# A macaron block on one core: the FFN weight prepared on VectorE alone, and the first five tiles' FFNs and values closer together

## The chip, the cores and the metric

The kernel runs on one core of one Trainium2 chip. The core has TensorE (PE, matrix products), VectorE (DVE), ScalarE (ACT) and GpSimd (POOL), and SyncE (SP), whose queue issues most transfers here. Each engine takes its instructions in the order in which they stand in its own queue and waits where an operand isn't ready. The metric is device time in microseconds of one launch; the smaller the better.

## The reference, cut to what matters

The input x has 4 batches of 4096 rows of 512 values, 16384 rows in all. Three residual steps follow one another:

```python
x = x + 0.5 * ffn(layernorm(x))
x = x + attention(layernorm(x))          # 16 heads of 32, each query sees 13 neighbouring keys
x = x + 0.5 * ffn(layernorm(x))
```

`ffn(x, w, b)` quantises both x and w before the product. Blocks of 32 neighbouring values get one scale, the largest absolute value over 7.5; each value over its scale goes to the nearest point of a six-bit floating grid (a tie to the lower one); the product is taken of grid point times scale. The FFN weight is 512 x 512, and both FFNs use the same one. Attention has a 1536 x 512 weight for query, key and value, a bias table of 25 offsets per head, and a 512 x 512 output weight.

## The kernel before

**Tiles and stages.** The 16384 rows are cut into 128 tiles of 128 rows. One tile goes through: the norm and quantisation for the first FFN (`quantised_norms`, kind "n1"), the first FFN and the attention norm (`first_half`), the values product (`values`), and later the output projection (`project_out`), the second quantised norm ("n3") and the second FFN (`second_half`). Four tiles make a group; per group and 128 columns there is an item m (128 of them): `project_qk`, `softmax`, `attend`. All products with a weight go through `product` (L146): 12 matmuls of 128 x 128 by 512, because both sides are held as a high and a low half in f16. The product names in the profile are pmf (FFN), pmv (values), pmqk (query and key), pmo (output), pmb (a bias through the output weight); ps and pv are the two attention products.

**What sets the order.** Stages are generators that are entered with `begin(slot, stage, rank)` in a list of numbered slots (L162); `run_slot` runs all that stand in one slot by rank, and each `yield n, rank` puts the rest of the stage n slots later. A tile has STEP = 7 slots. Tile t loads x at slot 7t-18, its first norm stands at 7t-10, its first half at 7t+5, its values at 7t+20; item m has its query and key products at 7m+38 and its softmax at 7m+42. From L779 on (`manual_schedule`) the order on each engine is the order in which the program is written. What stands ahead of that line, the setup up to the last FFN weight chunk and the first norms of tiles 0 to 2 (EARLY = 3), is put in order by a scheduler with a modelled timeline.

**The setup** (L629 to L872). SP loads the FFN weight `fw` in four chunks of 128 rows, the first x tiles, and 16 chunks `rows` of the other weights (order 8-11 value, 12-15 output, then query and key chunks in turns). ScalarE takes the sum of squares of every chunk. `powers(lo, hi)` makes from them, per weight, a power of two: a maximum on VectorE, a tiny transpose on TensorE (ptn), a maximum and a diagonal on VectorE, a tiny product on TensorE (pb), and some ten small integer operations on VectorE that end in `up` and `down`. For the FFN weight, `powers(4, 5)`; for the others, `powers(0, 4)` in slot 0.

The loop L745 prepares the FFN weight, chunk by chunk: VectorE makes wqh = fw / scale in f16; GpSimd makes wu = wqh times the high, then the low part of the scale, and VectorE takes each off fw; VectorE makes wq from the rest, adds wqh, breaks ties (`tie_to_lower`, L142 and L144); ScalarE rounds to fp8 (w8); GpSimd multiplies the scale back in (L766); ScalarE casts the high half, VectorE makes the low half (whlf, L769), and SP transposes it into `wt` (`put_weights`, L704). The 16 other chunks go through `put_scaled` (whl: ScalarE L784, VectorE L786, SP transpose) in the slots of L866. The FFN's products need all four FFN chunks, a values product the chunks 8-11, pmb (`attention_bias`, L813) the chunks 12-15.

**Buffers that matter here.** The high and low halves hlq (quantised norm) and hln (attention norm) have one buffer each (`hlp`, L100); whl and whlf share four; `ps_m`, the products' PSUM, has three. The bias table is built from `rd`, `shifted` and `mask`/`masks`, transfers on SP (L828 to L857).

Of the kernel before, what the change touches and what calls it, by code (L numbers as in the profile page):

```python
# [37 lines left out]
P = 128  # L38
# [12 lines left out]
QB = 32  # L51
# [13 lines left out]
def macaron_kernel(  # L65
# [66 lines left out]

    def blocks(t):
        return t.rearrange("p (n q) -> p n q", q=QB)

    def tie_to_lower(t):

        nc.vector.scalar_tensor_tensor(t, t, BELOW_ONE, t, ALU.mult, ALU.min)  # L142
        ti = t.bitcast(I32)
        nc.vector.tensor_scalar(ti, ti, 1, None, ALU.bitwise_or)  # L144

    def product(pm, lhs, rhs):  # L146

# [14 lines left out]
    def begin(slot, stage, rank=5):  # L162
        slots.setdefault(slot, []).append((rank, stage))
# [400 lines left out]

    F1, V, QK, SC, PV, OUT, F2 = 5, 2 * STEP + 6, 5 * STEP + 3, 6 * STEP, 8 * STEP + 3, 13 * STEP + 2, 12

    def add_bias(t, b):
        nc.gpsimd.tensor_tensor(xs[t], xs[t], b, ALU.add)  # L568

    def one(f, *args):  # L570
        f(*args)
        return
        yield
# [24 lines left out]

    for t in range(NT):
        k = t * STEP  # L600
        begin(k - 18, one(load, t), 0)
        enlist(k - 10, t, "n1")
        if not 0 < t < EARLY:
            begin(k - 11, one(moments, k - 10, t, "n1"), 1)
        begin(k + F1, first_half(t))
        begin(k + V, values(t))
        begin(k + F1, one(add_bias, t, half_ffn_b), 8)
        at = out_slot(t)
        begin(at - 5, one(add_bias, t, after_b), 8)
        enlist(at + 2, t, "n3")  # L610
        begin(at, project_out(t, at + 2))
        begin(at + 6 if t < LAST else second_slot(t) - 2, one(add_bias, t, half_ffn_b), 8)
        begin(second_slot(t), second_half(t))
    for slot in together:
        if slot >= EARLY * STEP - 10:
            begin(slot, quantised_norms(slot), 1)
    for m in range(n_items):
        k = m * STEP
# [10 lines left out]
    with tc.tile_pool(name="setup", bufs=1) as sp, tc.tile_pool(name="scratch", bufs=2) as scr:  # L629
# [8 lines left out]
        nc.gpsimd.memset(rp, 0.0)  # L638
        nc.scalar.dma_start(out=rp[:, QR - 1 : QR - 1 + NREL], in_=rpb)


        rows = {}

        sq = sp.tile([P, 5 * KC], F32, name="sq")
        first = min(slots)
        for slot in range(first, first + EARLY * STEP, STEP):
            run_slot(slot)
        for _ in quantised_norms(-10):
            pass
        chunks = (8, 9, 10, 11, 12, 13, 14, 15, 0, 4, 1, 5, 2, 6, 3, 7)  # L650
        for o in chunks:
            w, i = (qkv_w, o) if o < 3 * KC else (proj_w, o - 3 * KC)
            rows[o] = xp.tile([P, dim], F32, tag="x", name=f"rows{o}")
            nc.sync.dma_start(out=rows[o], in_=w[i * P : (i + 1) * P, :])
        for o in (*range(4 * KC, 5 * KC), *chunks):
            src = fw[:, o - 4 * KC, :] if o >= 4 * KC else rows[o]
            junk = scr.tile([P, dim], BF16, tag="junk", name=f"junk{o}")
            nc.scalar.activation(junk, src, AF.Square, accum_out=sq[:, o : o + 1])
        ptb = ps_m.tile([P, 512], F32, tag="mm", name="ptb")
        nc.tensor.transpose(ptb[:, : 3 * KC], b12, ident[: 3 * KC, : 3 * KC])  # L660
        bT = sp.tile([P, 3 * KC], F32, name="bT")
        nc.vector.tensor_copy(bT, ptb[:, : 3 * KC])
        b2 = sp.tile([P, 3 * KC], F32, name="b2")
        nc.vector.scalar_tensor_tensor(b2, bT, 2.0 ** -8, bT, ALU.mult, ALU.mult)
        nc.vector.tensor_tensor(sq[:, : 3 * KC], sq[:, : 3 * KC], b2, ALU.add)
        top5 = sp.tile([P, 5], F32, name="top5")
        up = sp.tile([P, 5], F32, name="up")
        down = sp.tile([P, 5], F32, name="down")
# [1 line left out]
        def powers(lo, hi):  # L670

            w = hi - lo
            nc.vector.tensor_reduce(
                top5[:, lo:hi], sq[:, lo * KC : hi * KC].rearrange("p (m c) -> p m c", c=KC),
                AX.X, ALU.max,
            )
            ptn = ps_m.tile([P, 512], F32, tag="mm", name=f"ptn{lo}")
            nc.tensor.transpose(ptn[:w, :P], top5[:, lo:hi], ident)
            most = sp.tile([w, 1], F32, name=f"most{lo}")
            nc.vector.tensor_reduce(most, ptn[:w, :P], AX.X, ALU.max)  # L680
            diag = sp.tile([w, w], F32, name=f"diag{lo}")
            nc.vector.tensor_scalar(diag, ident[:w, :w], most, 2.0, ALU.mult, ALU.mult)
            ones_w = sp.tile([w, P], F32, name=f"ones{lo}")
            nc.gpsimd.memset(ones_w, 1.0)
            pb = ps_m.tile([P, 512], F32, tag="mm", name=f"pb{lo}")
            nc.tensor.matmul(pb[:, :w], ones_w, diag, start=True, stop=True)
            e = sp.tile([P, w], I32, name=f"e{lo}")
            nc.vector.tensor_copy(e.bitcast(F32), pb[:, :w])
            nc.vector.tensor_scalar(e, e, 23, None, ALU.logical_shift_right)
            nc.vector.tensor_scalar(e, e, 131, None, ALU.add)  # L690
            nc.vector.tensor_scalar(e, e, 1, None, ALU.logical_shift_right)
            nc.vector.tensor_scalar(e, e, 97, None, ALU.max)
            u, d = up[:, lo:hi].bitcast(I32), down[:, lo:hi].bitcast(I32)
            nc.vector.tensor_scalar(u, e, -1, 264, ALU.mult, ALU.add)
            nc.vector.tensor_scalar(u, u, 23, None, ALU.logical_shift_left)
            nc.vector.tensor_scalar(d, e, -10, None, ALU.add)
            nc.vector.tensor_scalar(d, d, 23, None, ALU.logical_shift_left)

        powers(4, 5)
        nc.vector.tensor_scalar(cf, down[:, 4:5], 0.5 / XS, None, ALU.mult)  # L700
        nc.gpsimd.tensor_scalar(half_ffn_b, half_ffn_b, 0.5, None, ALU.mult)

        def put_weights(o, hl):
            return nc.sync.dma_start_transpose(  # L704
# [19 lines left out]
        for o in range(KC):  # L724
            nc.vector.tensor_reduce(
                w_abs[:, o * NB : (o + 1) * NB], blocks(fw[:, o, :]), AX.X, ALU.max,
                apply_absolute_value=True,
            )
        nc.vector.tensor_scalar(w_sc, w_abs, 1.0 / Q_MAX, None, ALU.mult)
        split_scale()  # L730
        nc.vector.scalar_tensor_tensor(w_abs, w_hi, -Q_MAX, w_abs, ALU.mult, ALU.add)
        nc.vector.scalar_tensor_tensor(w_abs, w_lo, -Q_MAX, w_abs, ALU.mult, ALU.add)
        nc.vector.scalar_tensor_tensor(w_sc, w_abs, 1.0 / Q_MAX, w_sc, ALU.mult, ALU.add)
        nc.vector.tensor_scalar(w_sc, w_sc, Q_EPS, None, ALU.max)
        nc.vector.reciprocal(w_r, w_sc)
        split_scale()
        w_back = small("w_back")
        nc.vector.tensor_scalar(w_back, w_sc, up[:, 4:5], F8_SCALE, ALU.mult, ALU.mult)

        def large(name, o, dt=F32):  # L740
            return scr.tile(
                [P, NB, QB], dt, tag=name, bufs=3 if name == "wu_" else KC, name=f"{name}{o}"
            )

        for o in range(KC):  # L745
            fwb = blocks(fw[:, o, :])

            def per(t):
                return bc(t[:, o * NB : (o + 1) * NB], QB)

            qh, q0 = large("wqh_", o, F16), large("wq0_", o)
            nc.vector.tensor_tensor(qh, fwb, per(w_r), ALU.mult)
            for i, b in enumerate((w_hi, w_lo)):
                u = large("wu_", f"{o}_{i}")
                nc.gpsimd.tensor_tensor(u, qh, per(b), ALU.mult)
                nc.vector.tensor_tensor(fwb, fwb, u, ALU.subtract)  # L756
            nc.vector.tensor_tensor(q0, fwb, per(w_r), ALU.mult)
            nc.vector.tensor_tensor(q0, q0, qh, ALU.add)
            q0f = q0.rearrange("p n q -> p (n q)")
            tie_to_lower(q0f)  # L760
            w8 = large("w8_", o, F8)
            nc.scalar.activation(
                w8.rearrange("p n q -> p (n q)"), q0f, AF.Copy, scale=1.0 / F8_SCALE,
                saturate=False,
            )
            nc.gpsimd.tensor_tensor(fwb, w8, per(w_back), ALU.mult)  # L766
            hl = scr.tile([P, 2, dim], F16, tag="whl", bufs=4, name=f"whlf{o}")
            nc.scalar.copy(hl[:, 0, :], fw[:, o, :])
            nc.vector.tensor_tensor(hl[:, 1, :], fw[:, o, :], hl[:, 0, :], ALU.subtract)  # L769
            put_weights(4 * KC + o, hl)  # L770

        for t in range(1, EARLY):
            moments(t * STEP - 10, t, "n1")
            for _ in quantised_norms(t * STEP - 10):
                pass

        ctx.enter_context(tc.manual_schedule())  # L779

        def put_scaled(o):
            s = up[:, o // KC : o // KC + 1]
# [10 lines left out]
        vb = sp.tile([P, KC], F32, name="vb")  # L793

        def scales():
            powers(0, 4)
            nc.vector.tensor_scalar(cp, sd[:, 2:3], sd[:, 3:4], 1.0 / XS, ALU.mult, ALU.mult)
            nc.vector.tensor_scalar(
                alpha, sd[:, 0:1], sd[:, 1:2], QSCALE * XS ** -2, ALU.mult, ALU.mult
# [62 lines left out]
                    masks[:, k : k + 1, :].to_broadcast([P, KC, KN]), ALU.mult, ALU.add,  # L862
                )

        begin(0, one(scales), 9)
        for slot, o in zip((2, 4, 5, 6, 10, 13, 16, 19, 21, 23, 25, 27, 29, 31, 33, 35), chunks):  # L866
            begin(slot, put_scaled(o), 9)
        begin(28, attention_bias(), 9)
        begin(26, one(put_table), 9)
        slot = first  # L870
        while slot < QK:
# [47 lines left out]
```

## Time and profile before

| | before |
|---|---|
| median of 3 runs | 2388.48 us (2378.66 to 2392.82) |
| the profiled execution, its own time | 2398.3 us |
| its span | 2396.5 us |
| TensorE busy | 2285.3 us, 95% |
| VectorE busy | 2020.8 us, 84% |
| GpSimd busy | 1990.2 us, 83% |
| ScalarE busy | 1329.8 us, 55% |
| first FFN product begins | 58.50 us |
| first query product begins | 107.18 us |

The page of a profile gives busy time by engine, the chain of work that ended last, and the costliest groups of instructions. A timeline lists one engine's instructions in order: start in us, duration in us, engine, line and operation, what is written and read, and in brackets how long the engine was idle before it and what ended that ("<-"). A transfer's row on SPq is its issue, not its landing; when it landed is read from who waited for it. Where two instructions follow one another without a gap, the rows overlap by some 0.08 us, so that the pace, start to start, is a little shorter than the duration.

### The profile page before, as it was taken

The numbers are of one execution on the slowest core, as the hardware profiler recorded it, in microseconds if no ns is written. First come the engines' busy times: TensorE is split into PE (matmuls) and PEld (weight loads), VectorE is DVE, ScalarE is ACT, GpSimd is POOL, SyncE is SP. The second block draws the span as 40 slices with busy tenths as digits, with TensorE's granted clock in tenths as the row PEclk, the third lists the DMA queues.
The fourth block names the chain that finished last, engine by engine and source line by source line (L and its number), as shares of the span: only waits on it lengthen the run. The fifth ranks groups of instructions, "written<-read, shape, count | busy, mean of one in ns | idle before, by whom it ended". The sixth has DMA issues, their size and how long they took to land.

```text
span 2396.5 us, 82360 instructions
## 1 busy us (share of the span) xinstructions
PE 2285.3 (95%) x35539; PEld 1118.5 (47%) x35539; DVE 2020.8 (84%) x3588; ACT 1329.8 (55%) x2080; POOL 1990.2 (83%) x2012
## 2 busy tenths in 40 slices
PE   0799999999999999999999999999999999999998
PEld 0344444444444444444444444444444444444443
DVE  8789888888888888888888888888888878888886
ACT  4466555555555555555555555555555555555542
POOL 5578888888888888888888888888888888888886
PEclk9899999999999999999999999999999999999999
DMA  5789788777777777777777778877777786777773
GB/s 153 143 151 155 159 164 159 159 148 151 150 155 158 158 142 150 148 155 156 164 147 149 148 159 161 156 159 146 150 151 158 158 158 131 149 150 152 137 116 108
DMA packets 925701, 360.59 MB, mean 150 GB/s; under 512 B 718876, under 2 KB 889752, under 8 KB 925336
## 3 DMA queue, kind: packets, MB, share of 16 engines
q1 hardware_dynamic: 924992, 354.79, 74.3%
q8 instruction: 278, 4.55, 0.8%
q10 hardware_dynamic: 344, 0.53, 0.1%
q14 instruction: 87, 0.71, 0.1%
HBM read 110.15 MB, written 67.29 MB: 74 GB/s over the span
## 4 chain that ended last, share of the span: by engine, by line
PE 92%; DVE 4%; issue 1%; DMA 1%; POOL 1%; ACT 1%; SPq 0%; DVEq 0%; POOLq 0%; ACTq 0%
PE pmqk L151 28%; PE pmf L151 26%; PE pmo L151 14%; PE pmv L151 14%; PE ps L437 7%; PE pv L507 3%; DVE fw L756 0%; DMA x<-hln 0%; DVE hlq L204 0%; DVE stn L180 0%; DVE whl L786 0%; DMA fw<-in_L_ffn_weight_dram 0%; DVE sc L239 0%; POOL yq L251 0%; DVE x L279 0%
## 5 line engine op out<-in xcount | busy, mean ns | idle before, releaser
L151 PE MATMUL pmf<-wt,xT 128*128 128x512 f16 x3048 | 703.2, 381 | 12.9 <-DMA xT<-hlq 10.3
L151 PE MATMUL pmqk<-x,wt 128*128 128x512 f16 x3072 | 709.3, 381 | 4.8 <-DMA x<-hln 4.6
L151 PEld LDWEIGHTS <-xT 128*128 128x128 f16 x3048 | 298.8, 98 | 377.1 <-DMA xT<-hlq 12.7
L151 PEld LDWEIGHTS <-wt 128*128 128x128 f16 x3072 | 290.6, 98 | 342.7 <-issue 10.4
L151 PE MATMUL pmo<-wt,ring 128*128 128x512 f16 x1536 | 360.5, 385 | 8.5 <-issue 8.5
L151 PE MATMUL pmv<-wt,x 128*128 128x512 f16 x1536 | 354.1, 380 | 4.9 <-DVE mvn L181 4.9
L246 POOL TENSOR_TENSOR yq<-yq,r 128x1024 f32<-128x1024 f32 (+1 forms) x141 | 246.7, 1750 | 131.1 <-DVE r L244 131.1
L568 POOL TENSOR_TENSOR x<-x,half_ffn_b 128x512 f32<-128x512 f32 x256 | 327.8, 1280 | 0.1
L279 DVE SCALAR_TENSOR_TENSOR x<-pmf,coef,x 128x512 f32<-128x512 f32 x256 | 179.7, 702 | 151.9 <-PE pmf L151 151.6
L534 ACT ACTIVATE ring<-pv 128x510 f16<-128x510 f32 (+8 forms) x224 | 82.6, 415 | 396.6 <-PE pv L507 396.6
L314 ACT CAST vt<-pmv 128x512 f16<-128x512 f32 x128 | 75.1, 587 | 389.2 <-PE pmv L151 389.2
L180 DVE BATCH_NORM_STATS2 stn<-x 128x6 f32<-128x512 f32 x384 | 265.4, 691 | 9.0 <-DMA x<-in_L_attn_x_dram 0.2
L251 POOL TENSOR_TENSOR yq<-q,sc 128x1024 f32<-128x1024 fp8e4 (+1 forms) x141 | 246.9, 1751 | 1.0 <-ACT q L249 1.0
L151 PEld LDWEIGHTS <-x 128*128 128x128 f16 x1536 | 150.7, 98 | 187.6 <-DMA x<-hln 5.4
L377 DVE SCALAR_TENSOR_TENSOR qk<-pmqk,qk_b,qk 128x512 f16<-128x512 f32 x256 | 190.7, 745 | 52.9 <-ACT qk L373 51.8
L151 PEld LDWEIGHTS <-ring 128*128 128x128 f16 x1536 | 141.6, 99 | 173.2 <-issue 19.9
L480 POOL TENSOR_TENSOR sf<-sf,total 128x714 f32<-128x714 f32 (+2 forms) x128 | 178.8, 1397 | 42.8 <-DVE total L478 22.9
L186 POOL TENSOR_SCALAR rsq<-mv 128x2 f32<-128x2 f32 (+1 forms) x141 | 130.0, 922 | 99.3 <-DVE mv L181 96.9
L249 ACT ACTIVATE q<-yq,nudge 128x1024 fp8e4<-128x1024 f32 (+1 forms) x141 | 150.3, 1066 | 112.0 <-POOL yq L246 103.8
L373 ACT ACTIVATE qk<-pmqk,qk_b 128x512 f16<-128x512 f32 x256 | 176.5, 689 | 52.2 <-PE pmqk L151 50.4
L233 ACT ACTIVATE yq<-x,nbq,rsq 128x512 f32<-128x512 f32 x254 | 193.6, 806 | 18.3 <-POOL nbq L192 17.6
L487 POOL TENSOR_TENSOR p<-sf,p 128x714 f16<-128x714 f32 (+2 forms) x128 | 192.8, 1506 | 0.1
(145 smaller groups left out, 3466.3 us busy)
## 6 DMA issues: line engine op xcount, KB each, us to landing
vs<-vd SPq DMA_DIRECT2D x144, 357.0 KB
x<-in_L_attn_x_dram SPq DMA_DIRECT2D x128, 256.0 KB
vd<-vt SPq DMA_DIRECT2D x128, 256.0 KB
out_dram<-x SPq DMA_DIRECT2D x128, 256.0 KB
vs<-vd SPq DMA_DIRECT2D x24, 378.0 KB
vs<-vd SPq DMA_DIRECT2D x24, 315.0 KB
rows<-in_L_attn_qkv_w_dram SPq DMA_DIRECT2D x12, 256.0 KB
xT<-hlq SPq DMA_TRANSPOSE x141
```

Source lines behind the costliest of these rows:

```text
L151: nc.tensor.matmul(pm, lhs(a, c), rhs(b, c), start=(n == 0), stop=(n == 3 * KC - 1))
L180: nc.vector.bn_stats(st, xs[t])
L233: nc.scalar.activation(y[:, u], xs[t], AF.Identity, bias=nb[:, u : u + 1], scale=rs[:, u : u + 1])
L246: nc.gpsimd.tensor_tensor(yb, yb, bc(r, QB), ALU.mult)
L251: nc.gpsimd.tensor_tensor(yb, q8.rearrange("p u (n q) -> p (u n) q", q=QB), bc(sc, QB), ALU.mult)
L279: nc.vector.scalar_tensor_tensor(xs[t], pm, cf, xs[t], ALU.mult, ALU.add)
L373: nc.scalar.activation(t[:, s, 0, KN:], pms[s], AF.Identity, bias=bias)
L377: nc.vector.scalar_tensor_tensor(t[:, s, 1, KN:], pms[s], bias, t[:, s, 0, KN:], ALU.add, ALU.subtract)
L437: nc.tensor.matmul(ps[rows, u, :sides, w * KN : (w + 1) * KN], t[rows, 0, part, q0 : q0 + QR], t[rows, 1, :sides, k0 : k0 + KN], start=par ...
L480: nc.gpsimd.tensor_tensor(s, s, bc(total[:, :n], KN), ALU.mult)
L487: nc.gpsimd.tensor_tensor(p[:, :n, KN : 2 * KN], s, ph, ALU.subtract)
L568: nc.gpsimd.tensor_tensor(xs[t], xs[t], b, ALU.add)
```

## The change

- All FFN weight work that GpSimd had (wu, and the product that multiplies the scale back) is on VectorE. The loop over chunks becomes a generator `quantise(o)`, and `both(o, n)` runs n steps of two chunks in turns: chunks 0 and 1, then 2 and 3. One line moves the halving of `half_ffn_b` from GpSimd to ScalarE.
- `manual_schedule` is entered at the start of the setup, so nothing is left to the scheduler. The first norms of tiles 0, 1 and 2 and the squares of the 16 chunks stand at written places between the steps of the weight's chunks. `powers` becomes a generator that yields twice (one slot each in slot 0 to 2). The mask building on GpSimd and the transfers of rd, shifted and masks now stand, as before in the text, behind all that, and so in every queue.
- The chunks' order is 8-11, then query and key in turns, then 12-15, and their slots change; `attention_bias` moves from slot 28 to 33.
- The first five tiles (SOON = 5): loads in slots -18 to -14, first norms in slots -10, -9, -8, 1 and 5, first halves in slots 5, 8, 11, 14 and 17, values eight slots behind each. Before, the first halves stood in slots 5, 12, 19, 26 and 33, and the values in 20, 27, 34, 41 and 48. Tiles from 5 on keep their slots; so do all items.

```diff
+    SOON = 5
+    def n1_slot(t):
+        if t < EARLY:
+            return t - 10
+        return t * STEP - 10 if t >= SOON else 4 * (t - EARLY) + 1
+    def first_slot(t):
+        return t * STEP + F1 if t >= SOON else 3 * t + F1
...
-        begin(k - 18, one(load, t), 0)
-        enlist(k - 10, t, "n1")
+        begin(k - 18 if t >= SOON else first_slot(0) - 23 + t, one(load, t), 0)
+        enlist(n1_slot(t), t, "n1")
...
-        begin(k + F1, first_half(t))
-        begin(k + V, values(t))
+        begin(first_slot(t), first_half(t))
+        begin(first_slot(t) + (V - F1 if t >= SOON else 8), values(t))
...
+        ctx.enter_context(tc.manual_schedule())
...
-        chunks = (8, 9, 10, 11, 12, 13, 14, 15, 0, 4, 1, 5, 2, 6, 3, 7)
+        chunks = (8, 9, 10, 11, 0, 4, 1, 5, 2, 6, 3, 7, 12, 13, 14, 15)
...
-        nc.gpsimd.tensor_scalar(half_ffn_b, half_ffn_b, 0.5, None, ALU.mult)
+        nc.scalar.activation(half_ffn_b, half_ffn_b, AF.Copy, scale=0.5)
...
-                u = large("wu_", f"{o}_{i}")
-                nc.gpsimd.tensor_tensor(u, qh, per(b), ALU.mult)
+                nc.vector.tensor_tensor(u, qh, per(b), ALU.mult)
+                yield
                 nc.vector.tensor_tensor(fwb, fwb, u, ALU.subtract)
+                yield
...
-            nc.gpsimd.tensor_tensor(fwb, w8, per(w_back), ALU.mult)
+            nc.vector.tensor_tensor(fwb, w8, per(w_back), ALU.mult)
...
+        ready = [quantise(o) for o in range(KC)]
+        def both(o, n):
+            for _ in range(n):
+                step(ready[o])
+                step(ready[o + 1])
+        step(norms[0])
+        both(0, 4)
+        step(norms[0])
+        for o in chunks[:4]:
+            square(o)
+        moments(n1_slot(1), 1, "n1")
+        both(0, 2)
+        step(norms[0])
+        step(norms[1], 2)
+        both(0, 3)
...
+        both(2, 1)
+        step(norms[1])
+        both(2, 1)
+        step(norms[1])
+        step(norms[2], 5)
+        nc.vector.tensor_tensor(sq[:, : 3 * KC], sq[:, : 3 * KC], b2, ALU.add)
...
-        begin(0, one(scales), 9)
-        for slot, o in zip((2, 4, 5, 6, 10, 13, 16, 19, 21, 23, 25, 27, 29, 31, 33, 35), chunks):
+        begin(0, scales(), 9)
+        for slot, o in zip((3, 4, 5, 6, 12, 15, 18, 20, 22, 24, 26, 28, 29, 30, 31, 32), chunks):
             begin(slot, put_scaled(o), 9)
-        begin(28, attention_bias(), 9)
+        begin(33, attention_bias(), 9)
```

## The prediction

> **What bounds the kernel now.** I read the page's busy line first, then TensorE's timeline to find where its idle time lies, then the timelines of the other queues there. By the page TensorE is the bound:
>
> ```profile
> PE 2285.3 (95%) x35539; PEld 1118.5 (47%) x35539; DVE 2020.8 (84%) x3588; ACT 1329.8 (55%) x2080; POOL 1990.2 (83%) x2012
> ```
>
> Span 2396.5 less 2285.3 leaves 111 us without a matmul. The change's places in TensorE's timeline (start, duration, what; in brackets the idle time before it and its releaser):
>
> ```profile
> 42.77 0.56 PE L686 MATMUL pb<-diag,ones 4*128 4x4 f32 x2 [5.75 <-DVE diag L682]
> 58.50 5.28 PE L151 MATMUL pmf<-wt,xT-10_160 128*128 128x512 f16 x12 [15.17 <-DMA wt<-whlf]
> 66.45 2.75 PE L151 MATMUL pmf<-wt,xT 128*128 128x512 f16 x12
> 74.10 4.45 PE L151 MATMUL pmv<-wt,x 128*128 128x512 f16 x12 [4.90 <-DVE mvn L181]
> 107.18 5.34 PE L151 MATMUL pmqk<-x,wt 128*128 128x512 f16 x24 [1.01 <-DMA x<-hln]
> ```
>
> Real work starts at S = 58.5, when the last FFN weight transpose lands. From the first pmqk (107.2) on, TensorE is nearly full, so the change is worth what it does to the start of pmqk of item 0, called T, less what moves out of the time behind T. Before S, VectorE is the long queue, and GpSimd slows it. VectorE's timeline, with GpSimd in products and without:
>
> ```profile
> 29.86 1.53 DVE L757 TENSOR_TENSOR wq<-fw,w_r 128x512 f32<-128x512 f32 x1
> 37.12 0.68 DVE L757 TENSOR_TENSOR wq<-fw,w_r 128x512 f32<-128x512 f32 x1
> ```
>
> GpSimd's timeline beside the first:
>
> ```profile
> 29.35 1.49 POOL L755 TENSOR_TENSOR wu<-wqh,w_hi 128x512 f32<-128x512 f16 x1
> ```
>
> The same operation takes 1.53 or 0.68; start to start 1.455 or 0.60. So a GpSimd product costs VectorE 0.855.
>
> **A. Up to the last FFN weight chunk.** Removed: 12 GpSimd products (8 L755, 4 L766). Added: 12 on VectorE at 0.60 (no row shows an fp8 or f16 input beside a broadcast there; nearest row L757). Sum in the changed program's order: the abs maxima end at 9.0; x0 lands at 9.75 and its moments end at 10.4; two tiny TensorE results are then waited for (ptn 0.37, pb 0.55, ptb 0.25), to 12.4; scale chain 2.0; norm 0's sc and r 1.15; a dozen dependent small operations at about 0.18, 1.9, plus 0.855 for one GpSimd product among them: the first wqh starts at 18.3 (now 15.2). From there 37 two-input operations and 4 L142 at 0.60, 4 L144 at 0.34, 2 moments at 0.7, 2 sc/r at 1.1 = 29.6, plus 4 GpSimd products of the first norms, 3.4. Last whlf: 18.3+29.6+3.4 = 51.3, now 54.83: 3.5 earlier. Bounds: start 16.5 to 19, GpSimd 2 to 4.5: 48 to 53.
>
> *The skill.* The Trainium skill, SBUF — State Buffer, section "SBUF: two separate sides", says the port that VectorE and GpSimd share is an exclusive lock, so the loser waits out the whole instruction; a pair would then take 0.60 + 1.04 = 1.64, and the 12 products removed would be worth 12.5. The row says 1.455 for a pair, 10.3 for twelve. I go by the row.
>
> **B. From there to TensorE.** This is where I expect the gain of A to be lost. TensorE's order puts the power chain of the other weights (ptn, pb of 4 columns) ahead of pmf 0; it now stands, on VectorE, behind the low half of tile 2's first norm. All norms share one hlq buffer:
>
> ```profile
> 42.81 0.62 ACT L200 CAST hlq-3_389<-yq-3_378 128x512 f16<-128x512 f32 x1 [0.21 <-DMA xT-10_160<-hlq-10_158]
> ```
>
> So tile 2's copy waits until tile 1's transpose has landed, and that one is queued behind both last weight transposes. After the last whlf: 0.75 and 1.3 for two SP issues, 3.25 to land (55.18 to 58.41 for whlf), copy 0.6, low half 0.7, x3's moments, bias add and maximum 1.1, ptn/most/diag/pb with handovers 1.6: 9.3. S = 60.6, now 58.5. Bounds 8 to 10: S 56 to 63. Sending half_ffn_b's halving to ScalarE costs nothing: ScalarE idles from 9.34 to 12.24. The two extra x loads delay the weight rows by some 1.1 us; their squares, spread over ScalarE's queue in groups of four to eight (0.62 each), are used only at the maximum near 59. GpSimd's mask building (1.6) moves behind tile 2's norm, near 54, and ends before x3's moments want GpSimd at 58.7; without that room it would delay tile 3's norm by as much.
>
> **C. To the end of the fifth values.** The rd, shifted and masks transfers move behind tile 2's transpose on SP, ahead of the V weights:
>
> ```profile
> 18.00 0.68 SPq L828 DMA_DIRECT2D rd<-rp  x1
> 23.36 1.77 SPq L831 DMA_DIRECT2D shifted<-rd  x4
> 25.23 2.45 SPq L857 DMA_DIRECT2D masks<-mask  x4
> ```
>
> They hold SP for some 7 to 9.7 us (about 59 to 68); V weights land near 76, just before they are needed. pmf 0 starts cold: 5.3, to 65.9. x0's add waits for GpSimd's bias add, which now stands behind tile 4's factors: r ends at 64.5, then 1.05+1.1+1.3 = 68.0, add 0.75. From there to hln 0 7.4 (now 63.8 to 70.8), landing 3.3 to 4.1: hln 0 at 79.9, S+19.3 (now S+15.6). Each next tile waits for its predecessor's hln transpose, since hln too has one buffer:
>
> ```profile
> 158.11 0.62 ACT L200 CAST hln<-yn 128x512 f16<-128x512 f32 x1 [1.23 <-DMA x<-hln]
> 102.95 4.10 DMA x<-hln
> ```
>
> (the second line is from the chain.) Per tile: copy 0.6, a whl on ScalarE 0.65 and VectorE 0.65, hln 0.6, a whl transpose ahead on SP 1.3, landing 3.3 to 4.1: 7.2 (bounds 6 and 8; now about 10). Three make 101.5; tile 4 has no whl in its chain, 5.0: 106.5. Its values run partly cold, 2.75 to 4.45: they end at E = 110. TensorE has only 5.5 of work per tile, so it idles in each.
>
> **D. To pmqk of item 0.** pmb needs all four projection chunks, now last of 16, and stands ahead of pmqk. ScalarE's and VectorE's orders put six whl behind the values of tile 4. After E: vt 1.3, table 0.95, sc/r 1.1, first whl 0.65, its issue and landing 3.7 to 4 (whl has four buffers, so the fifth of these six waits for the first), two whl ScalarE steps 2, yq and vbx 1.3, vbx and the last whl on VectorE 1.3: last low half at E+12.5; its transpose lands 3.3 later (the row: issued 108.23, GpSimd's memset released at 111.56): E+15.8. pmb now stalls too, but on less; its rows give the cold speed:
>
> ```profile
> 92.34 1.04 PE L151 MATMUL pmb<-wt,vbx 128*128 128x512 f16 x4 [1.20 <-ACT vbx L816]
> 96.59 3.59 PE L151 MATMUL pmb<-wt,vbx 128*128 128x512 f16 x8 [3.21 <-DVE vbx L817]
> ```
>
> 12 cold matmuls take 4.45 to 5.3; 4.9 gives T = E+20.7 = 130.7, now 107.2: 23.5 later. Bounds 13 to 18 for the wait.
>
> The Trainium skill, TensorE: Matmul & The Clock Gate, section "What's actually happening", has the array at half rate for about 3.4 us after an idle window of that length, some 1.7 lost per cold start, so pmb would take 4.4 and T would be 0.5 earlier. The rows 4.45 and 5.28 after idle, against 2.75, lose 1.7 to 2.5.
>
> **E. Behind T.** Two values products (2 x 2.7 = 5.4) leave the steps of items 0 and 1. VectorE is busy 11.2 of each 11.6 us step there, 10.6 without vt, against TensorE's 9.0, so by ps of item 1 I find 2.7 left; and pmqk of item 4 now waits 3.55 for a transpose that SP, working without a break since 126.5, issues at 153.62; SP loses only 0.4 (a vd store). Gain 0.5 to 5.4; I take 1.0, nearest to SP's row. Behind that the order is the same.
>
> **Sum.** +2.1 (S) + 21.4 (S to T: 70.1 against 48.7) - 1.0 = +22.5 on the profiled execution's 2398.3 (span 2396.5 and 1.8 around it): 2421. That execution was 9.8 above the median 2388.48, so on the median 2411.
>
> **Rivals.**
> 1. *The head costs only a little.* If A to D fall near their low ends (S 56.3, hln 0 at S+15.6, 6 per tile, 4.5 and 2.75 for tile 4, then 13 + 4.45), T is 114.6, and with E at 1 to 5.4 the change is +2 to +6; half way, +12, 2400. For it: most waits I add are of 1 to 4 us and some may overlap. Against: D alone has 11 us of ScalarE and VectorE work in a row, in which TensorE has nothing.
> 2. *Faster, because TensorE sets its own pace from S to T.* With S = 56.3 and 11 products at 2.75 plus one cold start of 2.5, T would be 89, -18, less 1: 2370. It decides where T falls below 107.2 + 1 - 12 = 96. For it: the FFNs and values of five tiles are ready work in a row, and tiles no longer wait for seven slots. Against: it needs tiles at 5.5 us, which the single hln buffer forbids (0.6 + 0.6 + 3.3 to 4.1 before anything else), and the last six whl ahead of tile 4's values, where the order has them behind.
> 3. *VectorE doesn't get quicker without GpSimd* (broadcast or mixed-type products stay at 1.455): 37 x 0.855 less the 3.4 counted = 28 more, 2439. Against: the 0.68 row above, whose operand is a broadcast too.
>
> **How the numbers follow.** The measurement tells about 0.5% (12 us) from no change. My forecast (slower by 12 to 30) 0.72; rival 1 (-12 to +12) 0.17; rival 2 0.06; rival 3 or other added waits above +30 0.05. Hence slower 0.77, same 0.17, faster 0.06. The forecast's own range, from bounds that seldom fall together (all low +2, all high +33), is +12 to +30: 2400 to 2418. To leave out no more than 2 in 10, with 5 us for the spread of the runs shown: 2393 to 2421.
>
> **What would show it.** In the profile after: two-input VectorE operations at 0.68 and no wu or fw rows on GpSimd (A); pmf 0 at 59 to 62 and released by the chain through pb, not by whlf (B); x<-hln transposes about 7 apart, TensorE idle some 7 us before pmv 0 and at half clock in the gaps (C); an idle stretch of 13 to 18 us before pmb, released by the last whl transpose, and pmqk at 125 to 136 (D); steps of 9 to 10.6 in items 0 and 1, then a wait again before pmqk of item 4 (E). I am wrong if pmb follows tile 4's values at once, or if S falls below 55.

## The result and the profile after

The changed kernel takes 2409.6 us (median of 6 executions, 2404.5 to 2414.45) against 2389.3 us (6 executions of the kernel before beside it): ratio 1.009, 95% interval 1.0064 to 1.0116, so about 20 us slower. The forecast was 2411 us in a range of 2393 to 2421. The profiled execution of the changed kernel has a span of 2412.1 us, that of the kernel before 2396.5.

The busy line of the changed kernel's page:

```profile
PE 2282.6 (95%) x35539; PEld 1117.7 (46%) x35539; DVE 2017.6 (84%) x3600; ACT 1330.2 (55%) x2081; POOL 1976.1 (82%) x1999
```

TensorE does the same work in the same busy time (2285.3 before) in a longer span: what was added is waiting. Where it lies is in TensorE's timeline of the changed kernel (start, duration, what, idle time before it and its releaser):

```profile
58.73 0.55 PE L684 MATMUL pb<-diag,ones 4*128 4x4 f32 x2 [0.72 <-DVE diag L682]
59.22 4.58 PE L141 MATMUL pmf<-wt,xT-10_324 128*128 128x512 f16 x12
79.93 4.47 PE L141 MATMUL pmv<-wt,x 128*128 128x512 f16 x12 [10.95 <-DMA x<-hln]
128.86 5.28 PE L141 MATMUL pmb<-wt,vbx 128*128 128x512 f16 x12 [19.09 <-DMA wt<-whl]
133.93 5.69 PE L141 MATMUL pmqk<-x,wt 128*128 128x512 f16 x24
181.98 4.44 PE L141 MATMUL pmqk<-x,wt 128*128 128x512 f16 x12 [4.15 <-DMA x<-hln]
```

The line of the kernel before that answers to the last one, pmqk of item 4:

```profile
158.07 5.23 PE L151 MATMUL pmqk<-x,wt 128*128 128x512 f16 x12 [3.55 <-DMA x<-hln]
```

The first FFN product S begins at 59.22 (58.50 before), released by the power chain through pb and not by the FFN weight. The first query product T begins at 133.93 (107.18 before), behind two long waits, 10.95 for the first hln and 19.09 for the last weight transpose. From pmqk of item 4 on, the order on TensorE is the same in all kernels here: it begins at 181.98 against 158.07. So the sum is +0.7 up to S, +26.0 from S to T, -2.8 from T to item 4: +23.9 where the prediction has +2.1 + 21.4 - 1.0 = +22.5. The spans differ by 15.6 and the medians by 20.3; what lies behind item 4 does not take the same time in each execution (last section).

VectorE's timeline of the changed kernel, an undisturbed pair of products of two chunks, a pair with one GpSimd product beside it, the last whlf pair, and tile 2's low half ("x2" is a group of two):

```profile
18.90 1.28 DVE L776 TENSOR_TENSOR wu<-wqh,w_hi 128x512 f32<-128x512 f16 x2
36.09 2.07 DVE L778 TENSOR_TENSOR fw<-fw,wu 128x512 f32<-128x512 f32 x2
48.71 1.45 DVE L801 TENSOR_TENSOR whlf<-fw,whlf 128x512 f16<-128x512 f32 x2
55.94 0.69 DVE L194 TENSOR_TENSOR hlq-8_415<-yq-8_366,hlq-8_415 128x512 f16<-128x512 f32 x1 [5.17 <-ACT hlq-8_415 L190]
```

### The profile page after: what moved, and what is told of

Read it like the earlier page. It is cut to its first block, busy times and chain, and to the rows that moved or that the text cites. A ratio compares the mean times of both kernels' runs of the same rounds, so it can differ in the third digit from the quotient of the medians.

```text
span 2412.1 us, 82340 instructions
## 1 busy us (share of the span) xinstructions
PE 2282.6 (95%) x35539; PEld 1117.7 (46%) x35539; DVE 2017.6 (84%) x3600; ACT 1330.2 (55%) x2081; POOL 1976.1 (82%) x1999
## 4 chain that ended last, share of the span: by engine, by line
PE 90%; DVE 5%; DMA 1%; POOL 1%; issue 1%; ACT 1%; SPq 0%; DVEq 0%; ACTq 0%; POOLq 0%
PE pmqk L141 27%; PE pmf L141 26%; PE pmo L141 14%; PE pmv L141 14%; PE ps L427 6%; PE pv L497 3%; DMA x<-hln 1%; DVE stn L170 0%; DVE hlq L194 0%; DVE qk L367 0%; POOL yq L236 0%; DVE sc L229 0%; DVE total L466 0%; DMA xT<-hlq 0%; DVE x L269 0%
## 5 line engine op out<-in xcount | busy, mean ns | idle before, releaser
L141 PEld LDWEIGHTS <-wt 128*128 128x128 f16 x3072 | 290.6, 98 | 343.6 <-issue 11.2
```

Source lines behind the costliest of these rows:

```text
L141: nc.tensor.matmul(pm, lhs(a, c), rhs(b, c), start=(n == 0), stop=(n == 3 * KC - 1))
```

## The experiments

A time marked "one" is of one execution and can't tell less than some 12 us, so there the timeline decides. S, T and item 4 are of one profiled execution each. Two kernels stand twice: between their two profiles T differs by 0.5 and 1.4, item 4 by 0.7 and 3.0, so that less than that is not told by one profile. "Spacing" is the mean distance of the issues of the five transposes x<-hln of tiles 0 to 4.

| kernel | S | T | pmqk of item 4 | time, us | ratio to before, 95% |
|---|---|---|---|---|---|
| before | 58.50 | 107.18 | 158.07 | 2389.3 | |
| after | 59.22 | 133.93 | 181.98 | 2409.6 | 1.0064 to 1.0116 |
| preparation only | 58.52 | 108.33 | 157.29 | 2388.8 | 0.9984 to 1.002 |
| tiles and slots only | 58.42 | 129.46 | 176.60 | 2414.1 | 1.0088 to 1.0136 |
| weight chunks earlier | 59.19 | 128.50 | 173.20 | 2398.3 | 1.0021 to 1.0071 |
| and the bias earlier | 59.33 | 118.91 | 173.24 | 2405.7 | 1.0042 to 1.0103 |
| weight chunks earlier, again | 59.59 | 128.04 | 172.48 | 2398.1 | 1.0017 to 1.0052 |
| and the bias earlier, again | 59.28 | 120.26 | 176.25 | 2400.4 | 1.0032 to 1.0071 |
| wu on GpSimd | 60.87 | 135.72 | 180.18 | 2415.8, one | |
| two hln buffers | 59.18 | 131.29 | 175.76 | 2409.4, one | |
| two hlq buffers | 56.05 | 130.75 | 174.77 | 2413.6, one | |
| values later | 59.21 | 130.54 | 175.20 | 2408.8, one | |
| values later, two hln buffers | 59.28 | 123.60 | 167.74 | 2405.1, one | |
| all of them, and rd earlier | 55.75 | 108.31 | 156.40 | 2382.1 | 0.9956 to 0.9988 |

**1. The change in two halves.** First the new preparation of the FFN weight alone, with the first five tiles as before:

```diff
-        return t * STEP + F1 if t >= SOON else 3 * t + F1
+        return t * STEP + F1
...
-        begin(first_slot(t) + (V - F1 if t >= SOON else 8), values(t))
+        begin(first_slot(t) + (V - F1), values(t))
...
-        begin(33, attention_bias(), 9)
+        begin(28, attention_bias(), 9)
```

with the first norms', loads' and chunks' places of before as well (the first chunk in slot 3 instead of 2).

> The changed weight preparation (VectorE alone, written order, the other transfers behind it), but tiles 0 to 4, the chunks' order, the whl slots (the first in slot 3 instead of 2) and the output bias as before the change. Theory (the preparation's gain is eaten by the hlq wait, and the loss lies in the tiles' half): first FFN product at 59 to 60, first query product at 107 to 112, time 2386 to 2397, no change against before within 0.3%. Rival (the written order of the setup is the loss): first query product after 125, time 2405 or more.

Then the other half: the setup of the kernel before, with the tiles', chunks' and bias's new places.

> The kernel before, with its setup in the scheduler's order and GpSimd's products, but the changed slots of tiles 0 to 4, of the weight chunks and of the output bias. Theory (the loss lies in the tiles' half: five tiles chained by one hln buffer, then six whl behind tile 4's values): first FFN product at 58 to 61, an idle stretch of 12 to 20 us before pmb, first query product at 125 to 135, time 2402 to 2414. Rival (the tiles' half is free or a gain): first query product at 107 or earlier, time 2391 or less.

The preparation alone changes nothing that can be measured (1.0002). The last whlf ends near 50.1 instead of 54.83, yet S stands at 58.52, a little before the 59 to 60 that were expected. The new places alone cost the whole loss (1.0112, at 2414.1 just above what was expected): T at 129.46. That T and item 4 are here 4.5 and 5.4 earlier than in the changed kernel doesn't show in the time; the two intervals overlap. TensorE's timeline of that kernel:

```profile
76.21 5.25 PE L151 MATMUL pmv<-wt,x 128*128 128x512 f16 x12 [7.02 <-DMA x<-hln]
124.77 4.85 PE L151 MATMUL pmb<-wt,vbx 128*128 128x512 f16 x12 [18.90 <-DMA wt<-whl]
```

The wait before pmb, 18.90, is the same as with the new preparation (19.09). The loss is in C and D, not in A.

**2. The weight chunks earlier (D).** The changed kernel with chunks 12-15 in slots 20 to 23 instead of 29 to 32:

```diff
-        for slot, o in zip((3, 4, 5, 6, 12, 15, 18, 20, 22, 24, 26, 28, 29, 30, 31, 32), chunks):
+        for slot, o in zip((3, 4, 5, 6, 9, 10, 12, 13, 15, 16, 18, 19, 20, 21, 22, 23), chunks):
```

> The changed kernel with the 16 weight chunks in slots 3, 4, 5, 6, 9, 10, 12, 13, 15, 16, 18, 19, 20, 21, 22, 23: all whl ahead of tile 4's values. Theory (D: the 19.1 us before pmb are the six whl behind tile 4's values): idle before pmb under 7 us, tile 4's values 2 to 6 us later because the whl now stand in the tiles' chain, first query product at 118 to 125 (133.9 in the changed kernel), time 2394 to 2403. Rival (the wait only moves into the tiles' chain): first query product after 130, time 2406 or more.

The time was hit, T (128.50) and the wait before pmb were not. The transposes were there; the next input was not:

```profile
123.41 5.30 PE L141 MATMUL pmb<-wt,vbx 128*128 128x512 f16 x12 [10.51 <-ACT vbx L885]
```

vbx stands on ScalarE behind the norms of tiles 5 and 6, so that a second wait of 10.5 lay under the first of 19. The next kernel moves the bias to slot 22 as well:

```diff
-        begin(33, attention_bias(), 9)
+        begin(22, attention_bias(), 9)
```

> Edits: the slots of the other weights' chunks moved earlier, as in the run before (last four chunks at slots 20 to 23), and now attention_bias at slot 22 instead of 33, so that its bias rows vbx no longer stand on ScalarE behind the norms of tiles 5 and 6. My theory (step D: what holds pmb is the place of its inputs in the written-out orders, first the last weight chunks, then vbx): pmb begins at 115 to 118, when the last weight transposes have landed, pmqk of item 0 at 119 to 123 (128.5 with the chunks alone, 133.9 in the changed kernel), time 2387 to 2396, that is 12 to 22 below the changed kernel. The rival (pmb is held by the values of the first tiles and the norms as such, wherever its inputs stand): pmqk of item 0 at 126 or later and the time at 2396 or more.

pmb begins at 116.33, as expected, and T falls to 118.91, 0.1 under what was expected; the time, 2405.7, does not follow (2387 to 2396 were expected). TensorE, and below it VectorE, of that kernel:

```profile
118.91 5.34 PE L141 MATMUL pmqk<-x,wt 128*128 128x512 f16 x24
128.59 5.12 PE L141 MATMUL pmf<-wt,xT 128*128 128x512 f16 x12 [4.33 <-DMA xT<-hlq]
```

```profile
119.12 0.75 DVE L891 SCALAR_TENSOR_TENSOR after_b<-pmb,coef,after_b 128x512 f32<-128x512 f32 x1 [0.77 <-PE pmb L141]
119.78 0.68 DVE L229 TENSOR_REDUCE sc<-yq 128x16 f32<-128x512 f32 x1
124.71 0.69 DVE L194 TENSOR_TENSOR hlq<-yq,hlq 128x512 f16<-128x512 f32 x1 [2.99 <-ACT hlq L190]
```

The first norm of tile 5 (sc, hlq) stands on VectorE behind tile 4's values and behind after_b, which waits for pmb. Its sc begins at 119.78, in the kernel without this edit at 116.24: of these 3.5, 2.0 come with the values (vt at 116.75 instead of 114.72) and 1.5 with after_b. So T is earlier and the norm later: pmf of tile 5, in the step of item 0, waits 4.33, and further waits follow: item 4 begins at 173.24, where it began at 173.20 without the edit. The 9.6 us won at T were given back within four items. As the medians still differed (2405.7 and 2398.3, on different chips), both kernels were run once more on one chip:

> The kernel with the earlier weight chunks once more, beside the one that has the earlier bias product as well, now on one chip. In their first profiles pmqk of item 4 began at 173.20 and 173.24, so that the order behind it, which is the same, began at the same time; yet the medians were 2398.3 and 2405.7, on different chips. Theory (what is decided at item 4 decides the time, and the rest is TensorE's waits for nothing that the profile shows, which come and go from execution to execution and chip to chip): the two medians lie within 5 of each other, item 4 at 173 to 174 in both. The rival (something behind item 4 differs): the other is again slower by 7 or more.

> The kernel with the earlier bias product once more, on the same chip as the run before it. Theory: median within 5 of that run's, pmqk of item 0 near 118.9, of item 4 at 173 to 174. The rival: slower than that run by 7 or more.

2398.05 and 2400.41, that is 2.4 apart, so the theory holds for the time. Item 4 began at 172.48 and 176.25, both outside the 173 to 174 that were expected, and T of the second at 120.26. So the gain at T is again lost by item 4, which here even begins 3.8 later.

**3. What one GpSimd product costs (A).** The changed kernel with the eight wu back on GpSimd:

```diff
-                nc.vector.tensor_tensor(u, qh, per(b), ALU.mult)
+                nc.gpsimd.tensor_tensor(u, qh, per(b), ALU.mult)
```

> The changed kernel with the eight wu products back on GpSimd, in the written order. Theory (a GpSimd product costs VectorE 0.855, more than the 0.60 that VectorE takes itself): last low half of the FFN weight ends 2 to 5 us later than the changed kernel's 50.2, two-input VectorE operations at about 1.5 beside the wu. Rival (GpSimd's work beside VectorE is free): it ends 8 x 0.6 = 4.8 us earlier, at about 45.4.

The last whlf ends at 51.80 instead of 50.16, 1.64 later, just under what was expected. VectorE's timeline of that kernel:

```profile
19.02 2.12 DVE L778 TENSOR_TENSOR fw<-fw,wu 128x512 f32<-128x512 f32 x2 [0.94 <-POOL wu L776]
33.06 3.00 DVE L801 TENSOR_TENSOR whlf<-fw,whlf 128x512 f16<-128x512 f32 x2
```

A pair of VectorE operations takes 1.28 alone, 2.12 with one GpSimd product beside it, 3.00 with two: 0.84 to 0.86 each. As the eight products take 0.60 each on VectorE, moving them should be worth 8 x (0.84 - 0.60) = 1.9 by these rows, an estimate; 1.64 was measured. (In two places VectorE stood idle 0.94 for a wu instead of being slowed by it, as the bracket of the first row shows.) The Trainium skill, SBUF — State Buffer, section "SBUF: two separate sides", has the loser wait out the whole instruction of the other; by the 1.04 that the prediction took for such an instruction a pair would take 2.32 and 3.36. These rows show less.

**4. The hlq buffer (B).** Two hlq buffers for the first norms of tiles 0 to 4:

```diff
-            hl = hlp.tile([P, 2, 2, dim], F16, tag="hlq", name=f"hlq{slot}")[:, :n]
+            first = tiles[0][1] == "n1" and tiles[0][0] < SOON
+            hl = (scr if first else hlp).tile([P, 2, 2, dim], F16, tag="hlq", bufs=2 if first else 1, name=f"hlq{slot}")[:, :n]
```

> Only edit: the high and low halves of the first norms of tiles 0 to 4 have two hlq buffers instead of one. My theory (step B: tile 2's high-half copy waits until tile 1's transpose has landed, the low half follows on VectorE, and the power chain of the other weights stands behind that): the copy of tile 2 no longer waits about 4.7 on ScalarE, and S, the first pmf, falls from 59.2 to 55 to 56.5; it is then released by the landing of the last FFN weight transpose (near 54) or by the shortened chain. pmqk of item 0 near 130.5 instead of 133.9. The rival (the chain is late because of what else stands on VectorE behind the last FFN weight chunk, not because of the buffer): S stays at 58.5 or later.

ScalarE's timeline of the changed kernel, and under it that of this one:

```profile
55.29 0.62 ACT L190 CAST hlq-8_415<-yq-8_366 128x512 f16<-128x512 f32 x1 [4.70 <-DMA xT-9_408<-hlq-9_402]
```

```profile
52.08 0.62 ACT L190 CAST hlq-8_415<-yq-8_366 128x512 f16<-128x512 f32 x1 [1.16 <-POOL yq-8_366 L241]
```

The copy of tile 2 no longer waits for tile 1's transpose, and S falls from 59.22 to 56.05, T to 130.75, both as expected. The one execution took 2413.6 us, which tells nothing at this size.

**5. What sets the pace of the first five tiles (C).** Two theories were at hand: the single hln buffer, and the written-out order, in which VectorE's update of x of tile t+3 (it needs a TensorE product that stands behind the values of tile t) stands ahead of the low half of hln of tile t+2. First two hln buffers alone:

```diff
-        hl = hlp.tile([P, 1, 2, dim], F16, tag="hln2", name=f"hln2_{t}")
+        hl = (scr if t < SOON else hlp).tile([P, 1, 2, dim], F16, tag="hln2", bufs=2 if t < SOON else 1, name=f"hln2_{t}")
```

> Only edit: the high and low halves of the attention norm of the first five tiles have two buffers instead of one. My theory (step C: one hln buffer sets the pace of tiles 0 to 4, because a tile's copy waits until its predecessor's transpose has landed): the transposes x<-hln of these tiles, 6.7 to 8.1 apart in the changed kernel, come 5.5 to 6 apart, values of tile 4 end near E = 105 (from 109.8), pmqk of item 0 begins at 127 to 130 (from 133.9). The rival (VectorE's written-out order sets the pace: the update of x of tile t+3, which waits for a TensorE product that stands behind the values of tile t, stands ahead of the low half of hln of tile t+2): spacing stays at 7 or more, pmqk of item 0 at 131 to 134, so a gain under 3. In both theories the time of one run changes by less than the measurement tells, so the timeline decides.

The spacing stays: 6.5 against 6.6, less than the 7 that the rival named, but not the 5.5 to 6 of my theory. T is 2.6 earlier, which the rival allows. Then the order alone, the hln buffer single again:

```diff
-        begin(first_slot(t) + (V - F1 if t >= SOON else 8), values(t))
+        begin(first_slot(t) + (V - F1 if t >= SOON else 14), values(t))
```

> Only edit: the values of the first five tiles stand 14 instead of 8 slots behind their first half, so that the FFN product of tile t+3, and with it the update of its x, stands ahead of the values product of tile t in TensorE's order. hln keeps its one buffer. The theory that is left after the run with two hln buffers (the written-out order sets the pace: landing of hln of tile t, its values, the FFN product of tile t+3, the update of its x on VectorE, and only then the low half of hln of tile t+2): the loop is gone, and the transposes x<-hln come 5 to 5.9 apart on the mean (6.6 in the changed kernel, 6.5 with two buffers). The rival (the work of ScalarE, VectorE and SP per tile sets the pace, whatever the order): 6.3 or more. In both, pmb still waits for the last weight transpose, pmqk of item 0 at 122 to 133, so the time of one run changes by less than the measurement tells.

This theory falls too, in this form: the spacing is 6.5, and the rival, the engines' work per tile, is not excluded yet. ScalarE's timeline shows why; with the order out of the way, the hln copies of tiles 2 and 3 wait for the predecessor's transpose:

```profile
86.54 0.62 ACT L190 CAST hln<-yn 128x512 f16<-128x512 f32 x1 [3.04 <-DMA x<-hln]
94.28 0.62 ACT L190 CAST hln<-yn 128x512 f16<-128x512 f32 x1 [4.03 <-DMA x<-hln]
```

So both edits together:

> Both earlier edits together and nothing else: two hln buffers for the first five tiles, and their values 14 instead of 8 slots behind the first half. Each alone left the mean spacing of the transposes x<-hln where it was (6.6 in the changed kernel, 6.5 and 6.5). Theory: two limits of nearly the same length stand side by side, the one hln buffer and the written-out order, so that taking one away leaves the other; with both gone the spacing falls to 5 to 5.9, and the last of the five transposes is issued at 97 to 100.5 (102.6 to 103.0 so far). The rival (the engines' work per tile): 6.3 or more, the last at 102 or later. pmb still waits for the last weight transpose: pmqk of item 0 at 122 to 130.

SP's timeline of that kernel (issues of the five transposes), the changed kernel's first and last below:

```profile
76.76 1.23 SPq L195 DMA_TRANSPOSE x<-hln  x1
82.80 1.28 SPq L195 DMA_TRANSPOSE x<-hln  x1
89.45 1.25 SPq L195 DMA_TRANSPOSE x<-hln  x1
93.19 1.23 SPq L195 DMA_TRANSPOSE x<-hln  x1
96.55 1.28 SPq L195 DMA_TRANSPOSE x<-hln  x1
```

```profile
76.69 1.23 SPq L195 DMA_TRANSPOSE x<-hln  x1
...
103.03 1.23 SPq L195 DMA_TRANSPOSE x<-hln  x1
```

The spacing falls to 4.95, slightly below what was expected, the last issue from 103.03 to 96.55, and T to 123.60, though pmb still waits 16.6 for the last weight transpose. Two limits of nearly the same length stood side by side: taking one away leaves the other. The engines' work per tile, which had to stay at 6.3 or more, is excluded as the limit.

**6. All waits at once.** Both double buffers, the earlier chunks, the later values; vbx formed at slot 8 and pmb 24 slots later; and the rd, shifted and masks transfers and the mask building ahead of the FFN weight's preparation (the cut leaves out the edits shown above):

```diff
+        rd = dram.tile([HEADS, QR, W], F32, tag="rd", name="rd")
...
         step(norms[0])
         both(0, 4)
...
-            yield 3, 9
+            yield 24, 9
...
-        begin(33, attention_bias(), 9)
+        begin(8, attention_bias(), 9)
```

> Several edits to the changed kernel at once, each aimed at one wait: two hlq and two hln buffers for the first five tiles; the chunk slots of the earlier run; the bias rows vbx at slot 8 and pmb 24 slots behind; the values of the first five tiles 14 instead of 8 slots behind their first half; the rd, shifted and masks transfers and the mask building ahead of the FFN weight's preparation. My theory (the head's loss is a chain of waits made by single buffers and by places in the written-out orders, not by work): S at 55 to 57, pmqk of item 0 at 100 to 113 (107.2 before, 133.9 in the changed kernel), and with the two values products that left items 0 and 1 a time of 2378 to 2392: equal to or up to 0.4% below the kernel before. The rival (the work of ScalarE and VectorE per tile sets the pace of the head, some 7 per tile on VectorE with the weight chunks between): pmqk of item 0 at 118 or later, time 2395 or more.

2382.1 us, ratio 0.9972 (0.9956 to 0.9988) to the kernel before, 27 us below the changed kernel: it beats both. TensorE's timeline:

```profile
55.75 5.30 PE L141 MATMUL pmf<-wt,xT-10_356 128*128 128x512 f16 x12
100.48 5.30 PE L141 MATMUL pmv<-wt,x 128*128 128x512 f16 x12 [3.55 <-DMA x<-hln]
105.58 2.90 PE L141 MATMUL pmb<-wt,vbx 128*128 128x512 f16 x12
108.31 5.34 PE L141 MATMUL pmqk<-x,wt 128*128 128x512 f16 x24
```

pmb follows the last values without a wait. T is near where it was before (107.18), and two more values products are done by then; at item 4, where the same work is done in both, it is 156.40 instead of 158.07. Several edits were made together, so that each one's share in these 27 us isn't known. Beside this kernel the one before took 2390.1 us (18 executions), so the gain is 8.0 us. Only 1.7 stand at item 4, less than two profiles of one kernel differed there, and where the rest comes from is not settled.

## Why the prediction was right

- **A, right in size, its start forecast 1.5 too late.** From the first wqh to the end of the last whlf 33.3 us passed, 33.0 were forecast; the four GpSimd products cost 3.5 in the pairs' rows (forecast 3.4). But the first wqh begins at 16.84, not 18.3. For a GpSimd product beside the small operations ahead of it 0.855 was counted; it ran from 15.45 to 16.5 and those operations, 0.15 each, went on at a pace of 0.19 beside it. The rest of the start was shorter by 0.6. VectorE's 1.28 a pair excludes rival 3, VectorE not quicker without GpSimd.
- **B, right.** The forecast was that the gain of A is lost in the power chain behind tile 2's norm: 9.3 from the last whlf to S; measured 9.06 (50.16 to 59.22). The cause is shown by the run with two hlq buffers.
- **C, right in its ends, its cause half right.** The first hln landed at 79.93 (79.9 forecast), though S was 1.4 earlier than forecast: from S to x0's add 8.2 passed instead of 7.4, and from the add's end to the landing 11.8 instead of 11.2. The fifth values ended at 109.76 (110). The first four transposes came 7.25 apart on the mean (7.2 forecast), the fifth 4.6 behind them (5.0). The step's sentence "each next tile waits for its predecessor's hln transpose, since hln too has one buffer" names one of two limits. The second, VectorE's order, was not seen; it would have held the pace at 6.5 without the first.
- **D, the mechanism right, one term too small.** The wait before pmb ran to E+19.1, with 15.8 forecast and 18 as the upper bound. The term "vt 1.3" let ScalarE begin vt as soon as the values ended. In the rows it could not:

```profile
111.49 0.81 ACT L223 ACTIVATE yq<-x,nbq,rsq 128x512 f32<-128x512 f32 x1 [3.32 <-POOL nbq L182]
112.21 0.56 ACT L304 CAST vt<-pmv 128x512 f16<-128x512 f32 x1
```

  yq of tile 5 stands ahead of tile 4's vt and waits through GpSimd for VectorE's moments of tile 5, which stand behind tile 3's vt. The profile's chain that ended last takes this way, from tile 3's vt over these moments to tile 4's vt. That is 2.45 from the end of the values (109.76) to vt. Of the remaining 0.9, 0.5 is the last transpose: from the end of its low half (125.03) to its landing (128.86) 3.8 passed instead of 3.3. From pmb to T 5.07 went by (4.9 forecast). The Trainium skill, TensorE: Matmul & The Clock Gate, section "What's actually happening", would make that 4.4, an estimate: at half clock for about 3.4 us, 1.7 would be lost. The pmb rows of the kernels in which it waits lose 1.8 to 2.55 (4.51 to 5.30 against 2.75), so the page's value stands just under the low end here.
- **E, too small.** The gain behind T was 2.8 instead of 1.0, inside the bounds. The steps shrank from 11.6 to 9.4 and 9.8, and pmqk of item 4 waits 4.15 for its hln as foreseen (3.55 before). SP's queue before did not work "without a break since 126.5", as the step has it: it issued nothing from 131.84 to 133.28.
- **The sum** at item 4 is +23.9 for +22.5: D's 3.5 too small (3.3 in the wait, 0.2 in pmb), less 0.2 by which the values ended early and 1.8 by which E was too small. That the median came within 1.4 of the forecast is in part luck: the errors of D and E have opposite signs, and the medians differ by 3.6 less than item 4, for reasons that lie behind it (last section). Rival 1, a head that costs only a little, needed T near 115 to 123; it was 133.9. Rival 2, TensorE at its own pace, needed T under 96; with all the named waits attacked at once it is 108.31.

## What to carry to other kernels

Where the order on each engine is written out, the start of a product is decided by what stands ahead of its inputs in the other queues; after moving it, list every input's place, since under the wait that ends last the next one is often almost as long (19.1 for the weight, then 10.5 for vbx; the hln buffer, then VectorE's order at the same 6.5). Take such limits away together, or the experiment with one of them says falsely that it doesn't matter. And measure a gain at the first point from which the order is the same: 9.6 us at T were gone four items later.

## What the runs showed that was not expected

Behind item 4 all kernels have the same order and the same work, yet its length in the profiled executions is 2219.5 to 2239.8 us. It goes with TensorE's "issue" waits, in which TensorE waits for no operand that the profile shows: 9 to 13 waits of up to 4.7 us each. Over the 14 profiles the two rise together, from 9.0 us of waits and 2220.0 behind item 4 to 20.4 and 2239.8. Two executions of the same kernel, the one with the earlier chunks, in TensorE's waits between 200 and 2290 us (product, line, releaser: us in total, times, longest). The first, 10.8 us of them in all, took 2398.3 us:

```profile
PE pmo L141 <- issue: 7.0, 3, 2.9
PE ps L427 <- issue: 2.2, 4, 1.1
```

The second, 15.8 us in all, took 2404.85 us, though its T was 0.5 earlier:

```profile
PE ps L427 <- issue: 8.7, 5, 4.5
PE pmo L141 <- issue: 5.1, 4, 1.7
```

In the kernel before it was 19.2 us of such waits and 2238.4 us behind item 4; in the last kernel 11.9 and 2219.5 (the first is the slowest execution of its kernel on record, the second the fastest of its). The difference in time is larger than in the waits, and after a long one the next product is slower: pmo took 4.45 instead of 2.75 behind a wait of 3.41 in the kernel before, with a granted clock of 0.66 from 832 to 837 us.

The traces say what TensorE waits for there: its own instructions. Every page has a DMA queue of the kind "instruction" with 278 packets of 16,384 bytes, one for every 256 of TensorE's 71,078 matmuls and weight loads. In the 14 traces, all 152 "issue" waits between 200 and 2290 us end at one and the same place in such a block of 256 instructions, 1.2 to 1.9 us after a packet of that queue has landed. In all 3602 blocks of that stretch the instruction at this place never starts sooner than 1.2 us after its packet; where the packet landed more than 1.9 us ahead, there is no such wait. Why some packets come late is not shown, and it wasn't tried to take these waits away. They go with the spread because of which one execution can't tell less than some 12 us here.
